# Two transformer layers on one core: the first MLP block made of units 0 and 1, units 6 and 7 alone at the end

## The chip, the cores and the metric

The kernel runs on one core of a Trainium2 chip. Its time is the device time of one execution in microseconds (us); the figure quoted is the median of three runs. One execution was profiled as well, and its trace gives each instruction's start and duration on TensorE (PE; its weight loads are listed apart as PEld), VectorE (DVE), ScalarE (ACT), GpSimd (POOL) and on the queue of SyncE (SP), which issues the DMAs.

## What is computed

The input is 32 sequences of 64 tokens with 512 features, a condition vector for each sequence, and positions. Two layers follow each other, all in float32.

Layer 0 normalises by the root of the mean square, scaled by a projection of the condition, and applies attention with 8 query heads of 64, one key and value head, and rotary angles from the given positions. It adds the result to x, normalises again with a second scale, and applies the gated MLP, whose middle has 2048 features:

```
x = x + attention(ada_rms(x, cond)) @ Wo.T
h = ada_rms(x, cond)
x = x + (silu(h @ Wg.T) * (h @ Wu.T)) @ Wd.T
```

Layer 1 is attention alone: a layer norm with scale and shift from the condition, 16 query heads of 32, keys and values of 4 heads through a latent of 128, a window mask that hides nothing within 64 tokens, a softmax, an output projection and the residual.

## The kernel before

**Units and blocks.** The 2048 tokens are eight units of 256 (four sequences each, `UT` = 256). Attention of both layers goes unit by unit: `attention0(u, room)` (line 689) is layer 0 up to the MLP's input, `attention1(u, room)` (line 858) is layer 1. The MLP of layer 0 goes by blocks of one or two units: `BLOCKS = ((0,), (1, 2), (3, 4), (5, 6), (7,))`.

**The MLP.** Each weight matrix is cut into eight sets of 2x2 quarters, and the 2x2 product is made with seven products in place of eight; this needs sums of weight quarters, sums of input quarters, and sums of the products. For each of 24 sets (gate, up and down, eight each) a block issues 7 x 2 matmul calls, and each float32 call stands in the trace as two instructions, so 28. Their moving operand has 256 columns if the block has two units and 128 if it has one; the weights are read whole either way. Products P1, P6, P5, P7 come first (`EARLIER`, `gate_up_first`), P2, P3, P4 later (`gate_up_last`); `partial`, `silu` and `gated` empty PSUM (L1063 to L1105), `down` adds to x.

**Weights.** Sets are read again for every block, through four slots (`MW` = 4). In the first block the quarters come from `in_wmlp`, and `sums_of_set` (L331 to L334) makes four sums of them: three on VectorE (on GpSimd for the first two sets) and one on GpSimd. The sums are written to HBM (`sums`, L342 and L344), 512 KB for each set as are the quarters read; later blocks read three quarters and four sums (`load_part`, L296 to L302).

**Sums of the input.** The last unit of a block makes T1, T3, T2 and T4 at the end of its `attention0` (L850 to L853) on VectorE. In a block of one unit they are of halves of its tokens, in a block of two they are of the two units. Product P1 needs only the first unit's h, P6 needs T2.

**The opening.** Units 0 and 1 are interleaved by hand before the planner starts. `FIRST` is a string: "a" takes the next piece of unit 0's `attention0`, "b" of unit 1's, "m" a piece of the modulations (projections of the condition), "i" issues two idle matmul calls on a constant, "r" a square root that brings the table of Sqrt into ScalarE, and "|" marks VectorE's latest instruction, behind which the sums of sets 2 to 4 must come. Within this loop TensorE keeps the order of issue; the other engines' order is settled by the scheduler of the tile framework, which goes by priority and by what is ready. Units 0 and 1 run in a "lean" form, with more, shorter pieces and statistics by quarters. A piece ends at each `yield cost, latency`.

**Angles.** Cosine and sine of units 0 and 1 are made first (`first_angles`); `angles(units, apart)` (L410) makes them for two units at a time in eight pieces of VectorE and ScalarE work (L424 and L428 to L449). `turning` walks over `TURNED`, units (2, 3), (4, 5), (6, 7), as a job of the planner. There is one buffer for positions.

**The planner.** After the opening, `Order.run` (L81) picks the next piece of the job that is furthest behind (`done / total`) and is ready. In round j the jobs are the block's MLP, `attention0` of the next block's units (`in_turn`), what is left of unit 1 (`ahead`) and of the angles, and from round 1 on `chain`, layer 1 of units 0 to 5 in turn; its total is 0.8 x 24 for each unit of the block before. A round ends when the MLP and the next block's `attention0` are done. Unit 6's layer 1 begins within the last round (four pieces), and the end is again a hand-written string, `LAST`, of units 6 and 7. Five buffers hold x, so x of units 5, 6 and 7 is loaded after layer 1 of units 0, 1 and 2.

Of the kernel before, what the change touches and what calls it, by code (L numbers as in the profile page):

```python
# [1 line left out]

# [1 line left out]

# [7 lines left out]
I32 = mybir.dt.int32  # L12
AF = mybir.ActivationFunctionType
ALU = mybir.AluOpType
# [30 lines left out]
TURN = (0.15911865234375, 3.628432750701904e-05, 6.4192136051133275e-09, 1.4247115856860781e-12)  # L45
ROUND = 12582912.0
WARM = 11
STAY = 13854 - 4 * 128 + 4 * 128 + 4 * 256 + 128 + 4 * 7 * 256 + 4 * 7 * 256
FIRST = "aaaaaaa bb a mm aa bb a bbb aa b mm a bb r aa a m b a bi m b i a | b".replace(" ", "")
EARLY = 4  # L50
TURNED = ((2, 3), (4, 5), (6, 7))
BLOCKS = ((0,), (1, 2), (3, 4), (5, 6), (7,))
GROUPS = ((0, 1, 2, 3), (4, 5, 6, 7))
H2 = 4
MODS = 4
# [76 lines left out]
def two_blocks(ctx: ExitStack, tc: tile.TileContext, a: dict, out: bass.AP):  # L132
# [87 lines left out]
    nc.gpsimd.memset(quarter, float(np.float32(np.pi / 2)))  # L220

    positions = []
    pos_slot = fixed([P, 2 * S])

    def load_positions(units):
        t = pos_slot.bitcast(I32)[:, : len(units) * S]
        nc.sync.dma_start(t, a["pos"][:, units[0] * S : (units[-1] + 1) * S])
        positions.append(t)

    first_loads = ExitStack()  # L230
    first_loads.enter_context(ordered(tc, mybir.EngineType.SP))
    load_positions((0, 1))
    small = fixed([P, C_ALL])
    nc.sync.dma_start(small, a["small"])
    condT = small[:, C_COND:C_VECS].rearrange("p (k b) -> p k b", b=B)
# [174 lines left out]
    def angles(units, apart):  # L410

        n = len(units) * S
        cols = slice(units[0] * S, units[0] * S + n)
        posi = positions.pop()
        big = work("many", [P, 10 * n], f"many_{units[0]}", 1)
        prods, rnds = (big[:, i * 5 * n : (i + 1) * 5 * n].rearrange("p (k c) -> p k c", c=n) for i in range(2))
        few = work("some", [P, 9 * n], f"some_{units[0]}", 1).rearrange("p (k c) -> p k c", c=n)
        posf, ang, lo, hi, acc, sign, f, size, sine = (few[:, k] for k in range(9))
        v, c = nc.vector, nc.scalar

        def group(*steps):
            with after(tc, mybir.EngineType.DVE, latest(tc, mybir.EngineType.DVE)):
                for op, *args in steps:
                    op(*args)  # L424
            return 0.0, apart

# [12 lines left out]
        yield group((v.tensor_tensor, prods, prods, rnds, ALU.subtract))  # L439
        yield group((v.tensor_reduce, acc, prods.rearrange("p k c -> p c k"), AX.X, ALU.add))  # L440
        yield group(
            (v.scalar_tensor_tensor, acc, lo, TURN[2], acc, ALU.mult, ALU.add),
            (v.scalar_tensor_tensor, acc, ang, TURN[3], acc, ALU.mult, ALU.add),
            (v.tensor_scalar, rnds[:, 0], acc, ROUND, ROUND, ALU.add, ALU.subtract),
            (v.tensor_tensor, f, acc, rnds[:, 0], ALU.subtract),
        )
        c.activation(size, f, AF.Abs)
        c.activation(angle[:, 0, cols], size, AF.Sin, scale=-TWO_PI, bias=quarter)
        c.activation(sine, f, AF.Sin, scale=TWO_PI)  # L449
        turned_units.update(units)  # L450
        yield group((v.tensor_tensor, angle[:, 1, cols], sine, sign, ALU.mult))

    def turning():
        for i, units in enumerate(TURNED):
            yield from angles(units, 4.0 if i else 2.0)
            if i + 1 < len(TURNED):
                load_positions(TURNED[i + 1])

    def first_angles(u):

# [132 lines left out]
    def rms(u, s, h, room, name):  # L593

        x = x_units[u]
        lean = "lean" in room
        sq = tile4(room, "h", f"sq_{name}") if lean else work("sq", [P, KC, UT], f"sq_{name}", 1)

        with after(tc, mybir.EngineType.Activation, roots[-1]) if name == "a2" else nullcontext():
            nc.scalar.activation(sq, x, AF.Square)  # L600
        if lean:
            parts = [sq[:, k] for k in range(KC)]
            c = KC // 2

# [83 lines left out]

    def attention0(u, room):
        kb, vb = kblk0[u % 2], vblk0[u % 2]  # L690
        lean = "lean" in room
        h = tile4(room, "h", f"h0_{u}")

        def query(i):

            q = abank(f"q0_{u}_{i}").rearrange("p (c t) -> p c t", c=2)
            for c in range(2):
                project(q[:, c], wqkv[i], slice(c * P, (c + 1) * P), h)
            two = [P, 2, UT]

            def turn(cos, sin):
# [14 lines left out]
        if lean:  # L716
# [8 lines left out]
            turn = query(0)  # L725
            yield 3.4, 0.0

        if lean:
# [1 line left out]
        else:  # L730
# [1 line left out]
        yield 1.0, 0.0  # L732

        qT = tile4(room, "qT", f"qT0_{u}")
        turn = turn or query(0)
        turn(cos, sin)
        yield 0.0 if lean else 3.4, 0.0

        kv = kv or keys_values()
        ku = work("u", [P, 512], f"ku_{u}")[:HD0, :UT]  # L740
        kw = work("v", [P, 512], f"kw_{u}")[:HD0, :UT]
        nc.vector.tensor_tensor(kw, kv[:HD0, :UT], sin[:HD0], ALU.mult)
        nc.vector.tensor_tensor(ku, kv[:HD0, :UT], cos[:HD0], ALU.mult)
        nc.vector.stream_shuffle(kw, kw, OTHER)

        vT = work("vT", [P, US, 2, S], f"vT_{u}", 1)
        twice = [HD0, US, 2, S]
        nc.vector.tensor_tensor(
            vT[HD0:],
            kv[HD0:, :UT].rearrange("p (b s) -> p b s", s=S).unsqueeze(2).to_broadcast(twice),  # L750
            r[HD0:].rearrange("p (b s) -> p b s", s=S).unsqueeze(2).to_broadcast(twice),
            ALU.mult,
        )

        ku, kw = (t.rearrange("p (b s) -> p b s", s=S) for t in (ku, kw))
        nc.vector.tensor_tensor(kb[:HD0], ku, kw, ALU.add)
        nc.scalar.copy(kb[HD0:], kb[:HD0])
        yield 0.0 if lean else 1.7, 0.0

        query(1)(cos, sin)  # L760
        yield 3.4, 0.0

        vt = abank(f"vt_{u}").rearrange("p (b d) -> p b d", d=P)
# [442 lines left out]
    homes["now"] = everywhere  # L1206
    for u in range(2):
        first_angles(u)
    positions.pop()
    for _ in modulation(0):  # L1210
        pass
    load_positions(TURNED[0])
    load_sets(2)
    load_mod(2)
    load_mod(3)

    first = work("p0", [P, 1024], "p0_0", 1)

    ahead = Job(attention0(1, {"ring": "1", "lean": True}), A0)
    streams = {  # L1220
        "a": attention0(0, {"ring": "0", "lean": True, "p": [first[:, :512], first[:, 512:]]}),
        "b": ahead.pieces,
        "m": other_mods(),
    }
    with ordered(tc, mybir.EngineType.PE):
        for name in FIRST:
# [7 lines left out]
                roots.append(latest(tc, mybir.EngineType.Activation))  # L1234
            else:
                next(streams[name], None)
    rest = [ahead, Job(turning(), 1.0)]
    for w, key in ((wq1, "wq1"), (wkd, "wkd"), (wkv1, "wkv1"), (wo1, "wo1")):
        nc.sync.dma_start(w, a[key])
    for u in range(2, XB):  # L1240
        load_x(u)
    combine(0)
    combine(1)
# [30 lines left out]
            if not n:  # L1274
                return

    def in_turn(units):
        for u in units:
            while u not in x_units or u not in turned_units:
                yield 0.0, 1.0  # L1280
            yield from attention0(u, {"ring": "0"})

    chain = Job(behind(), 0.8 * A1)
    for j, units in enumerate(BLOCKS):
        now = Job(mlp(j), M * len(units))
        jobs = [now, *rest]
        must = [now]
        if j == 0:
            must.append(ahead)
        if j + 1 < len(BLOCKS):  # L1290
            more = [u for u in BLOCKS[j + 1] if u > 1]
            must.append(Job(in_turn(more), A0 * len(more)))
            jobs.append(must[-1])
        if j == 1:
            jobs.append(chain)
# [108 lines left out]
```

## Time and profile before

| What | us |
|---|---|
| median of 3 runs (998.87 to 1000.03) | 999.79 |
| the profiled execution, its own time | 1000.52 |
| its span, first to last instruction | 998.7 |
| TensorE busy in the span (98%) | 975.1 |
| weight loads, beside the matmuls (85%) | 852.4 |
| VectorE busy (53%) | 530.1 |
| GpSimd busy (43%) | 428.2 |
| ScalarE busy (30%) | 302.0 |
| mean granted TensorE clock | 0.997 of full |
| moved by DMA, 132.23 MB | 132 GB/s over the span |

A busy share is a mean over stages that differ. The span falls into an opening (0 to 62.3 us, units 0 and 1), a first MLP block of one unit (to some 171 us, where the next block's first product appears; its last down product ends near 184), three blocks of two units (to 842.8), a last block of one unit (to 946.3) and a tail in which only layer 1 of units 6 and 7 is left. A matmul row in the timeline gives its start, how long the group took, line, operation, tiles, shape and count, and in brackets the idle time before it with what ended it. The matmuls of the MLP start 0.112 us apart with 128 columns and 0.216 us apart with 256.

### The profile page before, as it was taken

Reading aid. Unit: us, or ns where it says so; the run is one execution under the profiler, and the core shown is the slowest. Engines: PE = TensorE matmul, PEld = TensorE weight load, DVE = VectorE, ACT = ScalarE, POOL = GpSimd, SP = SyncE. Lnnn points to the kernel's source line nnn. Section 1 sums busy time; section 2 is a strip of 40 time slices with the busy share of each in tenths; the row PEclk is TensorE's granted clock in tenths of the full one; section 3 lists DMA queues with packets and bytes.
Section 4 is the critical chain, followed back from the end, with each engine's and each line's share of the span. In section 5 each row is a group of like instructions: output and inputs, shape, how many; then the busy total and the mean of one; then the engine's idle time right before and its main releaser. Section 6 shows DMA issues by size and latency. Waiting matters only on the chain.

```text
span 998.7 us, 17463 instructions
## 1 busy us (share of the span) xinstructions
PE 975.1 (98%) x6710; PEld 852.4 (85%) x6710; DVE 530.1 (53%) x1119; ACT 302.0 (30%) x560; POOL 428.2 (43%) x439
## 2 busy tenths in 40 slices
PE   8899988999999999999999999999999999999998
PEld 7788988888888888887888888888788889999986
DVE  5658787654373442655246372455334643654274
ACT  4453233223214210225214251222313330423132
POOL 3336257335433334435343352454325343844252
PEclk9999999999999999999999999999999999999999
DMA  7837376624222445223232234333323335745401
GB/s 269 310 117 239 130 248 196 208 92 134 69 69 80 137 139 173 90 80 110 78 108 88 73 132 138 115 106 106 96 86 105 132 109 168 246 149 190 138 1 43
DMA packets 82642, 132.23 MB, mean 132 GB/s; under 512 B 8832, under 2 KB 48512, under 8 KB 82176
## 3 DMA queue, kind: packets, MB, share of 16 engines
q1 hardware_dynamic: 82560, 131.12, 39.5%
q8 instruction: 53, 0.87, 0.4%
q14 instruction: 29, 0.24, 0.1%
HBM read 114.31 MB, written 16.78 MB: 131 GB/s over the span
## 4 chain that ended last, share of the span: by engine, by line
PE 87%; DMA 4%; DVE 3%; ACT 1%; POOL 1%; issue 1%; SPq 1%; POOLq 0%; DVEq 0%; ACTq 0%
PE gu L1048 38%; PE down L1048 17%; PE po L626 11%; PE q L626 10%; DMA stays<-in_wmlp 2%; PE pp L661 2%; PE sc L974 2%; PE lat L626 1%; PE kv L626 1%; ACT cT L815 1%; PE cx L805 1%; PE cx L1005 1%; PE sc L784 1%; DMA mod<-in_mod 1%; PE tab L494 1%
## 5 line engine op out<-in xcount | busy, mean ns | idle before, releaser
L1048 PE MATMUL gu<-h,stays 128*128 128x256 f32 (+1 forms) x1280 | 258.5, 340 | 5.9 <-issue 5.2
L1048 PEld LDWEIGHTS gu<-h,stays 128*128 128x128 f32 x1280 | 208.0, 191 | 30.4 <-issue 7.4
L1048 PE MATMUL down<-stays 128*128 128x256 f32 (+1 forms) x1120 | 208.4, 339 | 0.3 <-DVE stays L332 0.3
L1048 PE MATMUL gu<-hc,stays 128*128 128x256 f32 (+1 forms) x960 | 195.4, 338 | 2.8 <-DVE stays L332 2.8
L1048 PEld LDWEIGHTS down<-stays 128*128 128x128 f32 x1120 | 177.2, 190 | 22.4 <-issue 3.6
L1048 PEld LDWEIGHTS gu<-hc,stays 128*128 128x128 f32 x960 | 157.4, 191 | 18.4 <-DVE stays L332 3.0
L626 PE MATMUL q<-h,stays 128*128 128x256 f32 x480 | 110.7, 384 | 0.0
L626 PE MATMUL po<-cT,stays 128*128 128x256 f32 x480 | 107.9, 380 | 1.0 <-ACT cT L815 0.8
L1104 POOL TENSOR_TENSOR stays<-gate,stays 128x768 f32<-128x768 f32 (+1 forms) x40 | 53.8, 1346 | 114.7 <-DVE stays L1093 103.2
L626 PEld LDWEIGHTS po<-cT,stays 128*128 128x128 f32 x480 | 90.3, 190 | 14.4 <-ACT cT L815 2.4
L626 PEld LDWEIGHTS q<-h,stays 128*128 128x128 f32 x480 | 91.4, 192 | 12.6
L1063 ACT COPY e<-gu 128x256 f32<-128x256 f32 (+1 forms) x80 | 26.2, 328 | 172.5 <-PE gu L1048 169.7
L637 POOL TENSOR_TENSOR qT<-u_q,v_q 128x512 f32<-128x512 f32 x30 | 38.2, 1275 | 86.1 <-DVE v_q L636 82.9
L656 POOL TENSOR_TENSOR p<-p,sm 128x512 f32<-128x512 f32 x40 | 41.5, 1057 | 72.3 <-DVE sm L655 66.0
L682 DVE TENSOR_TENSOR x<-x,po 128x512 f32<-128x512 f32 x28 | 19.2, 686 | 90.7 <-PE po L626 90.7
L1064 DVE TENSOR_TENSOR u<-e,gu 128x256 f32<-128x256 f32 (+1 forms) x80 | 28.6, 358 | 53.2 <-ACT e L1063 53.0
L613 POOL TENSOR_TENSOR h<-x,stays 128x1024 f32<-128x1024 f32 x12 | 23.1, 1929 | 68.4 <-DVE x L682 38.4
L1105 POOL TENSOR_TENSOR stays<-stays 128x512 f32<-128x512 f32 (+1 forms) x40 | 45.0, 1126 | 2.9
L568 DVE RECIPROCAL stays<-stays 128x256 f32<-128x256 f32 (+1 forms) x23 | 35.4, 1540 | 19.7 <-ACT stays L567 19.5
L1065 DVE TENSOR_TENSOR w<-u,gu 128x256 f32<-128x256 f32 (+1 forms) x80 | 29.1, 364 | 30.8 <-PE gu L1048 29.6
L1151 POOL TENSOR_TENSOR x<-x,c 128x256 f32<-128x256 f32 x16 | 12.1, 758 | 74.3 <-DVE c L1138 74.3
L1093 DVE TENSOR_TENSOR gate<-gu,u 128x512 f32<-128x512 f32 (+1 forms) x40 | 23.3, 582 | 32.8 <-PE gu L1048 32.5
(230 smaller groups left out, 1266.2 us busy)
## 6 DMA issues: line engine op xcount, KB each, us to landing
stays<-sums SPq DMA_DIRECT2D x96, 384.0 KB, 3.0
stays<-in_wmlp SPq DMA_DIRECT2D x120, 256.0 KB, 2.9
stays<-in_wmlp SPq DMA_DIRECT2D x120, 128.0 KB, 2.5
stays<-sums SPq DMA_DIRECT2D x96, 128.0 KB, 2.3
sums<-stays SPq DMA_DIRECT2D x24, 384.0 KB, 3.8
mod<-in_mod SPq DMA_DIRECT2D x8, 512.0 KB, 6.3
x<-in_x SPq DMA_DIRECT2D x8, 512.0 KB, 6.2
a<-in_wmlp SPq DMA_DIRECT2D x24, 128.0 KB, 3.8
```

The source lines that it names most:

```text
L568: nc.vector.reciprocal(r, r)
L613: nc.gpsimd.tensor_tensor(by_seq(h), by_seq(x), per_seq(s, u), ALU.mult)
L626: nc.tensor.matmul(ps, w[:, k, cols], h[:, k, :], start=(k == 0), stop=(k == KC - 1))
L637: nc.gpsimd.tensor_tensor(dst, u, v, ALU.add)
L656: nc.gpsimd.tensor_tensor(p8, p8, sm.unsqueeze(2).to_broadcast(wide), ALU.mult)
L1048: nc.tensor.matmul(ps[REGION[p]][:, c], w[:, slot, cols], moving, start=opening and ps.opens(p, c, k), stop=p in LATER, skip_group_check=True,
L1063: nc.scalar.copy(e, ps[0])
L1064: nc.vector.tensor_tensor(u2, e, ps[1], ALU.add)
L1065: nc.vector.tensor_tensor(w2, u2, ps[2], ALU.add)
L1093: nc.vector.tensor_tensor(c12_21, ps.late_pair()[:, :, 0], u2.to_broadcast([P, 2, ht]), ALU.add)
L1104: e.tensor_tensor(act[:, 2:5], gate[:, 1:4], act[:, 2:5], ALU.mult)
L1105: e.tensor_tensor(act[:, 0:4:2], act[:, 2:4], act[:, 1:3], ALU.subtract)
```

## The change

The first block takes units 0 and 1, and the units alone are 6 and 7, both at the end. Unit 1's `attention0` ends within the opening. In its place the planner's round 0 has the rest of unit 2 and then unit 3, which `AHEAD` lists by round; rounds 1 and 2 prepare (4, 5) and (6, 7), and the last two rounds prepare nothing. The opening string has two new letters: "t" takes the eight pieces of the angles of units 2 and 3, and "c" takes six pieces of unit 2's `attention0`, to the first half of its second pair of queries. The string's two "i" are gone, and "|" stands ahead of unit 1's output.

Unit 2 runs in a "split" form: keys and values come before the first queries, and each pair of queries can be broken after its first half. It has its own two rows for its statistics (`own`). The order of instructions in other units is the same. The positions have two buffers, the second load stands among the first loads, and x of unit 2 is loaded right behind the modulation weights. In `angles`, Abs and the two Sin must come behind ScalarE's latest instruction; unit 2's second square no longer has to come behind the last root.

```diff
-FIRST = "aaaaaaa bb a mm aa bb a bbb aa b mm a bb r aa a m b a bi m b i a | b".replace(" ", "")
+FIRST = "aaaa ttt aaa bb a tttt mm aa t bb a bbb c aa b mm a bb r aa b c bb m a b c | b a b c b a b c m b c".replace(" ", "")
-BLOCKS = ((0,), (1, 2), (3, 4), (5, 6), (7,))
+BLOCKS = ((0, 1), (2, 3), (4, 5), (6,), (7,))
+AHEAD = ((3,), (4, 5), (6, 7), (), ())
...
-    pos_slot = fixed([P, 2 * S])
+    pos_slots = [fixed([P, 2 * S]) for i in range(2)]
...
     load_positions((0, 1))
+    load_positions(TURNED[0])
...
-        c.activation(size, f, AF.Abs)
-        c.activation(angle[:, 0, cols], size, AF.Sin, scale=-TWO_PI, bias=quarter)
-        c.activation(sine, f, AF.Sin, scale=TWO_PI)
+        with after(tc, mybir.EngineType.Activation, latest(tc, mybir.EngineType.Activation)):
+            c.activation(size, f, AF.Abs)
+            c.activation(angle[:, 0, cols], size, AF.Sin, scale=-TWO_PI, bias=quarter)
+            c.activation(sine, f, AF.Sin, scale=TWO_PI)
...
         for i, units in enumerate(TURNED):
-            yield from angles(units, 4.0 if i else 2.0)
-            if i + 1 < len(TURNED):
-                load_positions(TURNED[i + 1])
+            if i:
+                load_positions(units)
+                yield 0.0, 4.0
+            yield from angles(units, 4.0)
...
-        with after(tc, mybir.EngineType.Activation, roots[-1]) if name == "a2" else nullcontext():
-            nc.scalar.activation(sq, x, AF.Square)
+        nc.scalar.activation(sq, x, AF.Square)
...
                 project(q[:, c], wqkv[i], slice(c * P, (c + 1) * P), h)
+                if split and not c:
+                    yield 1.7, 0.0
...
+        if split:
+            vT = keys(keys_values())
+            yield 1.7, 0.0
+        turn = turn or (yield from query(0))
         turn(cos, sin)
         yield 0.0 if lean else 3.4, 0.0
...
+        if not split:
+            vT = keys(kv or keys_values())
+            yield 0.0 if lean else 1.7, 0.0
+
+        (yield from query(1))(cos, sin)
...
-    load_positions(TURNED[0])
     load_sets(2)
     load_mod(2)
     load_mod(3)
+    load_x(2)
...
+    own = [fixed([P, UT]) for i in range(2)]
...
+    turns = turning()
+    third = attention0(2, {"ring": "0", "split": True, "r": own})
...
-        "b": ahead.pieces,
+        "b": attention0(1, {"ring": "1", "lean": True}),
+        "c": third,
         "m": other_mods(),
+        "t": turns,
...
-    rest = [ahead, Job(turning(), 1.0)]
+    rest = [Job(turns, 1.0)]
...
-    for u in range(2, XB):
+    for u in range(3, XB):
         load_x(u)
...
-        if j == 0:
-            must.append(ahead)
-        if j + 1 < len(BLOCKS):
-            more = [u for u in BLOCKS[j + 1] if u > 1]
-            must.append(Job(in_turn(more), A0 * len(more)))
+        if AHEAD[j]:
+            more = in_turn(AHEAD[j])
+            if j == 0:
+                more = chain_of(third, more)
+            must.append(Job(more, A0 * len(AHEAD[j]) + 12.0 * (j == 0)))
             jobs.append(must[-1])
```

More of the change, by code (lines that the diff above doesn't have):

```diff
@@ L1 @@
 from contextlib import ExitStack, contextmanager, nullcontext
+from itertools import chain as chain_of
 import numpy as np
@@ L47 @@
 WARM = 11
[L48 to L49 removed]
+STAY = 13854 + 128 + 2 * 256 - 4 * 128 + 4 * 128 + 4 * 256 + 128 + 4 * 7 * 256 + 4 * 7 * 256
+FIRST = "aaaa ttt aaa bb a tttt mm aa t bb a bbb c aa b mm a bb r aa b c bb m a b c | b a b c b a b c m b c".replace(" ", "")
 EARLY = 4
 TURNED = ((2, 3), (4, 5), (6, 7))
[L52 removed]
+BLOCKS = ((0, 1), (2, 3), (4, 5), (6,), (7,))
+AHEAD = ((3,), (4, 5), (6, 7), (), ())
 GROUPS = ((0, 1, 2, 3), (4, 5, 6, 7))
@@ L222, in two_blocks @@
     positions = []
-    pos_slot = fixed([P, 2 * S])
+    pos_slots = [fixed([P, 2 * S]) for i in range(2)]
     def load_positions(units):
-        t = pos_slot.bitcast(I32)[:, : len(units) * S]
+        t = pos_slots[units[0] // 2 % 2].bitcast(I32)[:, : len(units) * S]
         nc.sync.dma_start(t, a["pos"][:, units[0] * S : (units[-1] + 1) * S])
@@ L413, in angles @@
         cols = slice(units[0] * S, units[0] * S + n)
-        posi = positions.pop()
+        posi = positions.pop(0)
         big = work("many", [P, 10 * n], f"many_{units[0]}", 1)
@@ L690, in attention0 @@
         kb, vb = kblk0[u % 2], vblk0[u % 2]
-        lean = "lean" in room
+        lean, split = "lean" in room, "split" in room
         h = tile4(room, "h", f"h0_{u}")
@@ L724, in attention0 @@
             yield 1.7, 0.0
-            turn = query(0)
+            turn = yield from query(0)
             yield 3.4, 0.0
@@ L734, in attention0, with keys @@
         qT = tile4(room, "qT", f"qT0_{u}")
-        turn = turn or query(0)
+        def keys(kv):
+            ku = work("u", [P, 512], f"ku_{u}")[:HD0, :UT]
+            kw = work("v", [P, 512], f"kw_{u}")[:HD0, :UT]
+            nc.vector.tensor_tensor(kw, kv[:HD0, :UT], sin[:HD0], ALU.mult)
+            nc.vector.tensor_tensor(ku, kv[:HD0, :UT], cos[:HD0], ALU.mult)
+            nc.vector.stream_shuffle(kw, kw, OTHER)
+            vT = work("vT", [P, US, 2, S], f"vT_{u}", 1)
+            twice = [HD0, US, 2, S]
+            nc.vector.tensor_tensor(
+                vT[HD0:],
+                kv[HD0:, :UT].rearrange("p (b s) -> p b s", s=S).unsqueeze(2).to_broadcast(twice),
+                r[HD0:].rearrange("p (b s) -> p b s", s=S).unsqueeze(2).to_broadcast(twice),
+                ALU.mult,
+            )
+            ku, kw = (t.rearrange("p (b s) -> p b s", s=S) for t in (ku, kw))
+            nc.vector.tensor_tensor(kb[:HD0], ku, kw, ALU.add)
+            nc.scalar.copy(kb[HD0:], kb[:HD0])
+            return vT
+        if split:
+            vT = keys(keys_values())
+            yield 1.7, 0.0
+        turn = turn or (yield from query(0))
         turn(cos, sin)
         yield 0.0 if lean else 3.4, 0.0
[L739 to L760, printed above, removed]
+        if not split:
+            vT = keys(kv or keys_values())
+            yield 0.0 if lean else 1.7, 0.0
+        (yield from query(1))(cos, sin)
         yield 3.4, 0.0
@@ L1208, in two_blocks @@
         first_angles(u)
-    positions.pop()
+    positions.pop(0)
     for _ in modulation(0):
         pass
-    load_positions(TURNED[0])
     load_sets(2)
@@ L1215, in two_blocks, with in_turn @@
     load_mod(3)
+    load_x(2)
     first = work("p0", [P, 1024], "p0_0", 1)
-    ahead = Job(attention0(1, {"ring": "1", "lean": True}), A0)
+    own = [fixed([P, UT]) for i in range(2)]
+    def in_turn(units):
+        for u in units:
+            while u not in x_units or u not in turned_units:
+                yield 0.0, 1.0
+            yield from attention0(u, {"ring": "0"})
+    turns = turning()
+    third = attention0(2, {"ring": "0", "split": True, "r": own})
     streams = {
         "a": attention0(0, {"ring": "0", "lean": True, "p": [first[:, :512], first[:, 512:]]}),
-        "b": ahead.pieces,
+        "b": attention0(1, {"ring": "1", "lean": True}),
+        "c": third,
         "m": other_mods(),
+        "t": turns,
     }
@@ L1236, in two_blocks @@
                 next(streams[name], None)
-    rest = [ahead, Job(turning(), 1.0)]
+    for pieces in (streams[name] for name in "abm"):
+        assert next(pieces, None) is None
+    rest = [Job(turns, 1.0)]
     for w, key in ((wq1, "wq1"), (wkd, "wkd"), (wkv1, "wkv1"), (wo1, "wo1")):
         nc.sync.dma_start(w, a[key])
-    for u in range(2, XB):
+    for u in range(3, XB):
         load_x(u)
@@ L1275, in some @@
                 return
[L1277 to L1281, printed above, removed]
     chain = Job(behind(), 0.8 * A1)
```

## The prediction

> **What bounds the kernel now.** I read the page first, then busy time by stage, then TensorE's instructions in order of time, then the chain that ended last.
>
> ```profile
> span 998.7 us, 17463 instructions
> ...
> PE 975.1 (98%) x6710; PEld 852.4 (85%) x6710; DVE 530.1 (53%) x1119; ACT 302.0 (30%) x560; POOL 428.2 (43%) x439
> ```
>
> TensorE bounds the whole, so a change can win only where PE is idle or slow. I cut the span at the first MLP matmul (62.3), where block (1,2)'s first matmul appears (171.3), and where the later blocks start; the last cut is the tail.
>
> ```profile
> core 0: us, PE busy (x) PEld busy (x) DVE busy (x) ACT busy (x) POOL busy (x), PEclk, DMA share, GB/s
> 0.00:62.30 62.30, 54.43 (x607) 44.50 (x607) 35.34 (x91) 29.77 (x69) 26.42 (x42) 0.97 0.69 244
> 62.30:171.30 109.00, 100.82 (x846) 95.16 (x847) 88.79 (x210) 38.26 (x88) 54.59 (x65) 0.98 0.60 198
> 171.30:392.00 220.70, 220.32 (x1295) 190.70 (x1295) 107.68 (x209) 56.47 (x95) 86.01 (x81) 1.00 0.38 124
> ```
>
> PE idles 7.9 us in the opening, 8.2 us in the first block and 0.4 us in the next; there DVE falls from 81% to 49%. The PE rows of the first block with a wait:
>
> ```profile
> 95.63 1.13 PE L1048 MATMUL gu<-h,stays 128*128 128x128 f32 x8 [1.71 <-issue]
> ...
> 130.51 1.16 PE L1048 MATMUL gu<-hc,stays 128*128 128x128 f32 x8 [2.76 <-DVE stays L332]
> ...
> 163.86 2.04 PE L1048 MATMUL gu<-h,stays 128*128 128x128 f32 x8 [2.64 <-issue]
> ```
>
> The bracket is the wait ahead of the row. With four smaller ones (0.25, 0.33, 0.49 and 0.28; the 0.70 at the block's start I count to the opening) the block loses 8.46 us. The chain says where the first two of the long ones come from:
>
> ```profile
> 90.05 4.56 DMA stays<-in_wmlp
> ...
> 124.71 4.40 DMA a<-in_wmlp
> ...
> 129.51 0.95 DVE stays L332
> ```
>
> A weight set lands, DVE makes its sums (L331 to L333), the matmul follows. For a single unit, a set is 28 matmuls of 128 columns, 3.1 us (PE rows 72 in 8.04 us, 0.112 each). In that time DVE owes it three sums (12.9, 11.0 and 13.9 us over 22 sets: 1.7 us) and its share of the emptying of PSUM: of L1064, L1065 and L1084, 0.29 each, one 0.42 and half a 0.28 (1.4 us). That is 3.1 us of DVE for 3.1 us of PE, with unit 2's attention and the angles on top; and 1 MB of DMA (512 KB in, 512 KB of sums out), 330 GB/s, where 198 were moved. The last wait also costs clock: the eight matmuls at 163.86 take 2.04 us instead of 1.05, and the granted clock over 163 to 167 us is 0.61, 1.6 us at no progress. Lost: 8.46 + 1.6 = **10.1 us**.
>
> **The change, part by part.** (1) *First block a pair.* A set is now 28 matmuls of 256 columns at 0.216 us (16 in 3.45), 6.05 us, while the three sums stay 1.7 us and the emptying becomes some 2.1 us (three of 0.42, one of 512 columns at 0.69, half of 0.42): 3.8 us of DVE in 6.05, and 1 MB in 6.05 us, 173 GB/s. Both stand below what 842.8 to 946.3 carries without a wait for weights (188 GB/s, shown at D). I keep 0.6 us of the 10.1: **-9.5**. Bounds: at worst the waits halve only, as the load does (-5); at best all go (-10.1). The number of single and paired blocks is unchanged (two and three), so PE's matmul work is the same.
>
> (2) *More work ahead of that MLP.* Moved before it: unit 1's output (32 x 0.216 = 6.9), its statistics and row (0.65 + 1.0), and of unit 2 the mean (0.43), tables (0.9), keys (1.73) and three quarters of the queries (24 x 0.216 = 5.2). 16.8 us move, none is added; the MLP starts near 79. Its two "i" (eight idle matmuls of 0.112) go: **-0.9**.
>
> (3) *Angles of units 2 and 3 in the opening.* The rows of one pass sum to 6.2 us of DVE (18.6 over three), ACT to some 3.6, with one more table load of 1.28 for Sin and one back to Exp. DVE idles 2.73 us before 20.2, 0.83 before 28.4, 1.85 before 30.6 and 3.17 before 38.1. The first three operations fit; the last four groups, 4.2 us, stand ahead of unit 0's softmax in 2.7 us of idle: 1.5 us late. Unit 1's queries and tables (31.0 to 37.8 on PE) hide it to the transposes at 37.83, which wait for POOL's product that ended at 36.97: **+0.5**. From below 0; without the cover 1.5 + 1.28 = +2.8.
>
> On the table: the trace has it at 28.01 for 1.28 us, and other loads are followed by their activation 0.01 to 0.02 us later. [...]
>
> (4) *The end of the opening.* Now the MLP's second product needs unit 1's sums: last projection, x (0.69), square (1.06), statistics (0.65), root (0.32), reciprocal (0.55), row (1.0), product (1.22), three subtractions of 512 columns (0.69 each): 7.6 us, and some eight hand-overs of about 0.15. Beside it PE has unit 2's half queries (3 x 1.73), unit 0's row (1.0), its own 1.65, a transpose (0.1) and the first product (4 x 0.216 = 0.9): 8.8 us against 8.8. I take 1.1 us of wait, and 0.9 where a context waits for its copy. Gone are the waits of 0.35 and 0.70 in unit 0's end: **+1.0**. Bounds: -1.0; or DVE first turns a query (2.1) and makes three sets' sums (3 x 1.7, since "|" lets them start earlier): 7.2 us of wait, the 0.9, and a halved clock of 1.6 as at 163, less the 1.05: +8.7.
>
> On the clock: over 31 to 36 us it is 0.69, after a longest idle of 1.28. [...]
>
> (5) *Units 6 and 7 alone, one after the other.* The block of unit 6 carries two second-layer attentions (units 4 and 5) in some 115 us instead of 210 to 240. The single block now (842.8 to 946.3) shows what one costs: waits for POOL of 0.32 and 0.67. One attention more beside a single block: **+1.0**, bounds 0 to 3. That chain is long in latency, but the next MLP does not wait for it. Loads of x for units 5 to 7 hang on the attentions of units 0 to 2, which run with the same shares as units 1 and 2 do now (loads at 504 and 617, a wait of 0.74): nothing.
>
> (6) *Second position buffer, unit 2's own rows, loads moved on SP* (x of unit 2, positions): x already starts at 28.8 and is used after 40; the weights behind it are wanted at 79. Nothing; at worst the 6.2 us of one x landing, hidden by the later start. No change of the sum.
>
> **Sum.** -9.5 - 0.9 + 0.5 + 1.0 + 1.0 = -7.9. The profiled execution took 1000.52 (span 998.7): 992.6. The median of the runs is 0.73 lower, so **991.9**.
>
> **Rivals.** *A, the forecast* (0.57): 988.5 to 995.5.
>
> *B, the opening's end is exposed* (0.15): part (4) at its upper bound, 991.9 + 7.7 = 999.6, from 996 to 1003. For it: DVE is in every link and the order of its queue is not fixed here; against: in unit 0's end the same links leave PE waiting 1.05.
>
> *C, the opening gains* (0.12): unit 2's work also fills the older waits (28.05, 30.04, 45.24 and 47.77: 0.41 + 1.28 + 0.78 + 0.67 = 3.1) and the halved clock at 31 goes (1.6), and part (4) costs nothing: 991.9 - 4.7 - 1.0 = 986.2. Against: most unit 2 pieces come after 45 us.
>
> *E, the change doesn't do what it says* (0.08): the first block's waits hang on the order of loads and sums and not on the rate, 5 us stay: 991.9 + 4.5 = 996.4.
>
> *D, slower* (0.08): unit 7's block is starved of weights. It loses filler: of 28 us (103.5 less 24 x 3.14) I expect 10 to remain, unit 6's early pieces (costs of 3.5) and what is left of units 4 and 5 (costs of 45, of which the planner places 38.4 before). So 24 sets of 0.92 MB, 22.0 MB, are wanted in 75 + 10 = 85 us. Four sets are in the slots; 18.3 MB must land in about 82 us, 223 GB/s. The stage now averages 188; were that a ceiling, the block would take 15 us more: 1007. It undoes the gain below 203 GB/s. Against it:
>
> ```profile
> 842.80:946.30 103.50, 102.52 (x888) 98.12 (x887) 49.44 (x124) 29.19 (x64) 52.19 (x62) 1.00 0.58 188
> 860.00:870.00 10.00, 9.04 (x75) 8.39 (x74) 7.22 (x11) 6.08 (x10) 7.99 (x9) 1.00 0.84 271
> ```
>
> At 188 GB/s the queues are 58% busy, at 271 84%, and PE waited for no weights.
>
> **Numbers.** A measurement tells 0.2%, 2.0 us, from no change: faster is below 997.8, slower above 1001.8. Faster: A 0.57, C 0.12, E 0.06, B 0.04, together 0.79. Same: B 0.08, E 0.02, D 0.01: 0.11. Slower: B 0.03, D 0.07: 0.10. Range 986.5 to 1000.5: left out are half of C (0.06), B's top (0.05) and D (0.08).
>
> **What would show it.** Right: the MLP starts near 79; the first block (about 145 + 12 + 20 us) shows PE idle under 1.5 us, no L331 to L333 in front of PE, full clock. (3) is wrong if unit 0's transposes come later than 38.5; (4) if PE waits over 2 us for DVE's h or hc at the first MLP; (5) if the last two blocks idle over 3 us. The forecast fails if the clock halves at the MLP's start or the weights of unit 7 appear in the chain.

## The result, and the profile after

| What | before | after |
|---|---|---|
| median of the runs compared, us | 999.91 (6 runs, 998.87 to 1002.44) | 1006.92 (6 runs, 1004.7 to 1009.15) |
| ratio after to before, 95% interval | | 1.0067 [1.0047, 1.0086] |
| the profiled execution, us (its span) | 1000.52 (998.7) | 1006.68 (1004.9) |

The change makes the kernel slower, by 7.0 us; the forecast was 8 us faster, and the time lies above the whole range. The page after:

```profile
span 1004.9 us, 17433 instructions
...
PE 977.5 (97%) x6702; PEld 851.0 (85%) x6702; DVE 537.9 (54%) x1119; ACT 303.9 (30%) x562; POOL 426.9 (42%) x439
```

The work is the same, less eight idle matmuls. Of the 6.2 us that the span grew by, 2.4 stand in PE's busy time and 3.8 in its idle time. By stage (us; busy time and count of PE, PEld, DVE, ACT, POOL; granted clock, DMA share, GB/s), cut at the first MLP matmul of each block, and the first block at 256, where its weight sums end:

```profile
0.00:79.90 79.90, 69.12 (x712) 57.84 (x713) 53.98 (x126) 37.68 (x87) 30.59 (x46) 0.98 0.60 208
79.90:256.00 176.10, 168.65 (x915) 142.55 (x914) 119.40 (x222) 48.17 (x89) 81.92 (x78) 0.99 0.36 118
...
271.20:509.20 238.00, 237.08 (x1414) 202.05 (x1413) 117.51 (x224) 74.84 (x117) 99.90 (x91) 1.00 0.33 102
```

In the first block PE still idles 7.5 us, with DVE busy 68% of the time (82% before, over 62.3 to 182.3) and 118 GB/s moved (203 before). Both loads fell as forecast, and the waits stayed.

Idle time alone leaves out slow clock, and that matmuls right behind a wait took longer (four of 256 columns 1.13 us at 189.17, 1.03 at 187.15). So I took every matmul's distance to the next one's start, less the distance at which the same form streams undisturbed (0.216 us for 256 columns, 0.112 for 128; the fastest seen for the others), and summed this **loss** by stage. All losses below are counted so.

| Loss, us | before | after | difference |
|---|---|---|---|
| opening | 15.6 | 17.4 | +1.8 |
| first block | 14.1 | 13.9 | -0.2 |
| the four blocks behind | 3.5, 7.8, 2.4, 2.0 (15.7) | 7.4, 8.2, 1.8, 2.3 (19.7) | +4.0 |
| tail | 6.8 | 8.0 | +1.2 |
| idle matmuls dropped | | | -0.9 |

The sum is +5.9, the spans differ by 6.2. Four of PE's ten waits in the first block, the three longest among them (the bracket is the wait ahead of the row):

```profile
184.46 1.13 PE L1062 MATMUL gu<-h,stays 128*128 128x256 f32 x4 [0.59 <-DVE x L1167]
...
189.17 1.13 PE L1062 MATMUL gu<-h,stays 128*128 128x256 f32 x4 [0.99 <-DVE u L1078]
191.31 1.10 PE L1062 MATMUL gu<-h,stays 128*128 128x256 f32 x4 [1.01 <-DVE gate L1098]
...
252.61 5.60 PE L1062 MATMUL down<-stays 128*128 128x256 f32 x17 [2.02 <-DVE stays L335]
```

PE's waits there are all put down to DVE, and of their 7.5 us only 2.0 to a sum of weights (L335); the rest is the emptying of PSUM (L1078, L1098, L1107, L1116) and the addition to x (L1167). What DVE itself waited for, in the first block of the kernel before (62 to 184 us) and after (80 to 257; total, times, longest):

```profile
DVE stays L331 <- DMA stays<-in_wmlp: 8.7, 6, 2.2
DVE stays L333 <- DMA a<-in_wmlp: 3.8, 4, 2.0
```

```profile
DVE stays L334 <- DMA stays<-in_wmlp: 23.8, 17, 3.9
```

DVE stands for 23.8 us at the first sum of a set whose quarters have not landed. Its instructions there, in order:

```profile
186.52 0.43 DVE L334 TENSOR_TENSOR stays<-a,stays 128x256 f32<-128x256 f32 x1 [1.45 <-DMA stays<-in_wmlp]
186.98 0.43 DVE L335 TENSOR_TENSOR stays<-stays 128x256 f32<-128x256 f32 x1
187.32 1.27 DVE L658 TENSOR_REDUCE sm<-p 128x8 f32<-128x512 f32 x2
188.51 0.32 DVE L659 RECIPROCAL sm<-sm 128x8 f32<-128x8 f32 x2
188.75 0.37 DVE L1078 TENSOR_TENSOR u<-e,gu 128x256 f32<-128x256 f32 x1
...
246.88 0.43 DVE L334 TENSOR_TENSOR stays<-a,stays 128x256 f32<-128x256 f32 x1 [3.92 <-DMA stays<-in_wmlp]
...
247.82 0.69 DVE L1107 TENSOR_TENSOR stays<-gu,u 128x512 f32<-128x512 f32 x1
...
250.98 1.48 DVE L335 TENSOR_TENSOR stays<-stays 128x256 f32<-128x256 f32 x1
```

The rows show DVE keeping the order of its queue: at 246.88 it has stood for 3.92 us, and L1107, whose products PE had finished at 243.3, comes only behind the sum. L335 of the same set follows at 250.98, and PE waits 2.02 us for it. At 186.52 less was held up: ScalarE's exponentials, which the softmax's sum (L658) reads, ended at 186.08 and 186.60, and its copy for the emptying (L1078) at 186.86. So only 0.4 of the 1.45 us held ready work, and L334 and L335 themselves held it up to 187.3; PE then waited 0.99 for L1078 and 1.01 for L1098. Nobody needed that sum yet: counted by 28 MLP matmuls a set, its set begins on PE at 201.15. I call this distance, from the start of a set's first sum to the set's first matmul, its lead; its median over sets 2 to 23 is 12.0 us here and 4.9 in the kernel before.

The chain of waits tells why the quarters are late (start, length, what):

```profile
176.57 3.86 DMA stays<-in_wmlp
180.46 0.44 DVE stays L334
180.92 0.44 DVE stays L335
181.48 0.80 POOL stays L337
182.70 3.79 DMA stays<-in_wmlp
186.52 0.44 DVE stays L334
```

Two rows of SP's queue between them:

```profile
182.29 0.32 SPq L345 DMA_DIRECT2D sums<-stays  x1
182.70 0.41 SPq L303 DMA_DIRECT2D stays<-in_wmlp  x1
```

This turn reads as a ring: a load lands, the sums are made, their write is issued (L345), and behind it on the same queue the next load (L303), which takes 3.8 us. One turn takes 6.06 us, as long as a set on PE (6.05).

**Theory:** the first block loses its time to the order on DVE's queue. A sum is put ahead of work that is due, and waits there for a landing. **Rivals:** DVE is too busy; the DMA can't carry it; the moved pieces in the opening cost it.

### The profile page after: what moved, and what is told of

It is laid out like the page before. It is cut to its first block, busy times and chain, and to the rows that moved or that the text cites. A ratio compares the mean times of both kernels' runs of the same rounds, so it can differ in the third digit from the quotient of the medians.

```text
span 1004.9 us, 17433 instructions
## 1 busy us (share of the span) xinstructions
PE 977.5 (97%) x6702; PEld 851.0 (85%) x6702; DVE 537.9 (54%) x1119; ACT 303.9 (30%) x562; POOL 426.9 (42%) x439
## 4 chain that ended last, share of the span: by engine, by line
PE 85%; DVE 6%; DMA 4%; ACT 2%; POOL 1%; issue 1%; SPq 0%; POOLq 0%; DVEq 0%; ACTq 0%
PE gu L1062 35%; PE down L1062 17%; PE q L630 11%; PE po L630 10%; DMA stays<-in_wmlp 2%; PE pp L665 2%; PE sc L988 2%; PE lat L630 1%; PE kv L630 1%; PE cx L819 1%; PE cx L1019 1%; DMA stays<-in_wqkv 1%; ACT cT L829 1%; DVE stays L334 1%; PE tab L499 1%
## 5 line engine op out<-in xcount | busy, mean ns | idle before, releaser
L630 PEld LDWEIGHTS q<-h,stays 128*128 128x128 f32 x480 | 91.2, 192 | 12.5
L641 POOL TENSOR_TENSOR qT<-u_q,v_q 128x512 f32<-128x512 f32 x30 | 38.2, 1275 | 78.0 <-DVE v_q L640 70.6
L686 DVE TENSOR_TENSOR x<-x,po 128x512 f32<-128x512 f32 x28 | 19.2, 686 | 81.7 <-PE po L630 81.6
L1078 DVE TENSOR_TENSOR u<-e,gu 128x256 f32<-128x256 f32 (+1 forms) x80 | 28.8, 360 | 62.9 <-ACT e L1077 62.8
L1167 DVE TENSOR_TENSOR x<-x,down 128x256 f32<-128x256 f32 x48 | 18.0, 416 | 43.7 <-PE down L1062 43.7
L1169 POOL TENSOR_TENSOR x<-x,u_d 128x256 f32<-128x256 f32 x32 | 22.4, 725 | 40.2 <-DVE x L1167 40.1
```

The lines of the kernel that those rows point to most:

```text
L630: nc.tensor.matmul(ps, w[:, k, cols], h[:, k, :], start=(k == 0), stop=(k == KC - 1))
L641: nc.gpsimd.tensor_tensor(dst, u, v, ALU.add)
L1078: nc.vector.tensor_tensor(u2, e, ps[1], ALU.add)
L1169: nc.gpsimd.tensor_tensor(to, to, more, ALU.add)
```

## The experiments

Where nothing else is said, a diff is against the kernel after. "Waits for landings" are those of DVE at the first sum in the first block (80 to 257 us).

**The sums one set later.** The three places that call for sums ask for one set less ahead.

```diff
-        combine(place[what] + 2)
+        combine(place[what] + 1)
...
-                    combine(place[what] + 3)
+                    combine(place[what] + 2)
```

> Theory 1 (an in-order queue): in the first block VectorE stands at the sums of a set whose quarters have not landed yet, and the emptying of PSUM behind it makes TensorE wait; the planner issues the sums two sets ahead, just behind the product that frees the slot. Theory 2 (work): VectorE and ScalarE have too much to do in bursts there, attention and angles beside the sums. Here the sums are issued one set later, all work unchanged. Theory 1: VectorE's waits for landing quarters fall from 23.8 us to under 6, the first block loses 5 to 7 us in place of 13.9, time 998 to 1001. Theory 2: nothing is taken away, 1005 to 1008.

1004.76 us, 1.0058 [1.0036, 1.0079]. Waits for landings 21.5, first block 10.4. The call comes later, but the scheduler, free to order DVE, put the sums back to the same places: the median lead is 12.0 us, as without the edit. The edit failed to do what it was for; it tells only that the place of the call isn't the place in the queue.

**Sums of data that are already there**, and **no sums at all**. The first keeps every instruction and DMA and reads a resident weight in the place of the quarters; the second loads the slots of the sums by DMA.

```diff
-            e.tensor_tensor(f[:, 0], a21, l[:, 1], ALU.add)
...
+            w0, w1, w2, w3 = (wo0[:, k, :256] for k in range(4))
+            e.tensor_tensor(f[:, 0], w0, w1, ALU.add)
```

> The first block's sums are made from weights that lie in SBUF from the opening on (output weights of layer 0) in place of the set's own quarters, so the products of the MLP are not the reference's; the same instructions in the same places and the same DMAs, but no wait for a landing. Theory 1: 998 to 1001, as with the later issue. Theory 2: 1005 to 1008, since VectorE does the same work.

> The first block's sums are left out (0.42 us or more each, three on VectorE and one on GpSimd for each of 24 sets), and the four quarters that they would fill are loaded by DMA instead, as later blocks load them. Theory 1: 997 to 1000, little better than the two kernels that only take the wait away. Theory 2: about a third of VectorE's work in the block is gone, 1002 to 1005. If the first block were bounded by DMA: 1007 or more, since 128 KB a set more are moved.

Resident: 999.06, 0.9996 [0.998, 1.0012]. Its first block, over the same window as above:

```profile
79.90:256.00 176.10, 174.21 (x960) 149.82 (x959) 128.11 (x233) 48.72 (x91) 84.03 (x79) 1.00 0.33 115
```

DVE is busier (128 us for 119, as the block got further), the DMA moves as much (115 GB/s), and PE idles 1.9 us in place of 7.5. The block loses 4.9 for 13.9: 9.0 us, near the 9.5 of the forecast. The kernel's time shows less of it, as its opening loses 20.6 with a loss of 5.18 behind POOL at 30.0. Without sums: 993.14, 0.9937 [0.9915, 0.9959], first block 2.0, so 2.9 us are what the sums cost by being there (I had expected 997 or more). A busy DVE and a full DMA are refuted for this block; the wait for landings is left.

**The new blocks alone.** The blocks of after with the opening of before (and the rest of unit 1 behind it); units 2 and 3 and the angles wholly in the planner.

```diff
-FIRST = "aaaa ttt aaa bb a tttt mm aa t bb a bbb c aa b mm a bb r aa b c bb m a b c | b a b c b a b c m b c".replace(" ", "")
+FIRST = "aaaaaaa bb a mm aa bb a bbb aa b mm a bb r aa a m b a bi m b i a b bbbbb |".replace(" ", "")
-AHEAD = ((3,), (4, 5), (6, 7), (), ())
+AHEAD = ((2, 3), (4, 5), (6, 7), (), ())
```

> The new blocks alone: the opening has only units 0 and 1 (with the two pairs of idle matmuls), then unit 1's last pieces without cover; unit 2 and the angles of units 2 and 3 are left to the planner. Theory 1: the first block still loses 13 us or more, the end of the opening some 4 to 7 more than with unit 2's pieces beside it: 1009 to 1014. Theory 2, or if the angles and unit 2's pieces in the opening are what costs: 1000 to 1006.

1006.43, 1.0077 [1.0053, 1.0101]: the same as after. I expected it slower. The opening loses 18.1, the first block 15.2, each some 1 us more than after. That reads as if the moved pieces were worth nothing; two kernels further down show otherwise.

**The writes of the sums on another queue**: on GpSimd's, and on ScalarE's, so that no load stands behind a write.

```diff
-                nc.sync.dma_start(to[:, 0:3], sets["f"][n][:, 0:3])
+                nc.scalar.dma_start(to[:, 0:3], sets["f"][n][:, 0:3])
```

> Why do the quarters land late? Theory 1a: SyncE's queue is in order too, and the writes of a set's sums to HBM (which wait for VectorE and GpSimd) stand ahead of the loads of other sets, so that landing, sums, write and next load form a ring of about 6 us a set, as long as the 6.05 us of TensorE. Theory 1b: the loads wait for TensorE to free the slot, and VectorE's queue has the sums too early for what is loaded so late. Here the writes are issued by GpSimd. 1a: the first block loses 5 to 8 us in place of 13.9, time 998 to 1002, if issuing costs GpSimd no more than 1 us a write. 1b: 1004 to 1008.

> The same writes issued by ScalarE. 1a: SyncE's loads are free, but ScalarE's queue now stands before writes that wait for the sums, with the copies that empty PSUM behind them: between 998 and 1005. 1b: 1004 to 1008.

On ScalarE: 1003.06, 1.003 [1.0018, 1.0043], first block 9.7.

```profile
DVE stays L334 <- DMA stays<-in_wmlp: 17.2, 16, 2.2
```

On GpSimd: waits for landings 14.6, first block 12.5, opening 23.0; 1009.83, 1.0094 [1.0066, 1.0122]. The waits fall by a quarter to two fifths: the shared queue of SP is a part of the ring, not its whole. On GpSimd the time lies above both expectations: PE still waits 2.5 for DVE's L1098, it waits 1.97 at 161.2 for a statistic that GpSimd makes (L561), and the opening loses 5.6 more than after.

**The sums late, and held there.** The calls of the first experiment, and each sum must come behind DVE's latest instruction at its call.

```diff
-            with after(tc, mybir.EngineType.DVE, marks[0]) if 2 <= n < 5 else nullcontext():
+            with after(tc, mybir.EngineType.DVE, latest(tc, mybir.EngineType.DVE)) if n >= 2 else nullcontext():
```

> The sums one set later, and besides each set's sums must stand behind VectorE's instructions that were issued before them, so that the scheduler can't move them forward. Theory 1 in either form: VectorE's waits for landings fall under 8 us of 23.8, the first block loses 5 to 8 us: 998 to 1001. If a later place makes TensorE wait for the sums themselves, the wait comes back as matmuls behind L335: 1003 to 1008.

995.85, 0.9961 [0.9947, 0.9976]. DVE's waits for landings in the first block (80 to 247 us), and its window up to where the sums end:

```profile
DVE stays L334 <- DMA stays<-in_wmlp: 2.1, 1, 2.1
```

```profile
79.80:245.80 166.00, 164.73 (x913) 141.93 (x912) 116.97 (x226) 48.38 (x89) 80.99 (x79) 1.00 0.40 130
```

The waits go, the median lead falls to 5.4 us, the stretch with the same sums takes 166.0 us in place of 176.1, and the block loses 3.8: 10.3 less than before the change. The other stages stay as in after (17.3; 7.5, 7.5, 1.8, 2.3; 8.0). No instruction was taken away and the loads of quarters take no less (a median of 3.0 us for 256 KB in both): the order alone was worth 11 us (10.6 by the ratios to the kernel before, which ran beside each). This version beats both kernels.

**All sums on GpSimd.**

```diff
-            e = nc.gpsimd if n < 2 else nc.vector
+            e = nc.gpsimd
```

> All sums of the first block on GpSimd (0.64 us each instead of 0.42). Theory 1: VectorE no longer stands in front of a landing, GpSimd does, and behind it stand the products that only the later down projection needs: 995 to 1001. Theory 2, or if GpSimd becomes the bound (82 us busy of 177, some 42 more): 1003 to 1010.

1005.11, 1.005 [1.0032, 1.0069], first block 10.1. The same wait has moved to the other queue (GpSimd's waits, 80 to 257 us):

```profile
POOL stays L334 <- DMA stays<-in_wmlp: 21.8, 9, 4.3
```

PE no longer waits for the emptying on DVE. It waits 3.2 us for the statistic of L561, behind GpSimd's queue, and the granted clock behind it is 0.57 over 155 to 159 us. The theory had 995 to 1001; the time fell where the rival had it, because GpSimd's queue too holds work that PE waits for.

**The same order in the kernel before**, that is, with one unit in the first block (later calls and held sums, against the kernel before).

> The kernel before with its own blocks and opening, and only the sums' new place (one set later, fixed behind what VectorE was given before). If the queue's order is the whole cause, its first block too falls from 14.1 us of loss to 5 or less: 990 to 993. If the rate argument of the prediction holds beside it (3.1 us of VectorE for 3.1 us of TensorE with a unit alone), the first block keeps 9 us or more: 994 to 1000.

1004.81, 1.0045 [1.0029, 1.0061]: slower, and above both expectations. The landing waits fall to 1.3, yet the first block loses 19.2 for 14.1. PE's waits there (60 to 188 us):

```profile
PE pp L661 <- POOL p L656: 3.1, 2, 2.6
PE gu L1048 <- issue: 3.0, 1, 3.0
PE gu L1048 <- ACT some L449: 1.7, 1, 1.7
```

Here DVE is busy 105.1 of 126.4 us (83%). The median lead is only 1.6 us; PE waits behind the softmax's product (L656), for 3.0 us that the profile puts to no engine, and behind ScalarE's work on the angles (L449), and the granted clock is 0.75 over 129 to 133 us and 0.69 over 167 to 171. So this order gains nothing in a block of one unit. That agrees with what the forecast said of the rate, but does not prove it: no other order was tried there.

**The new blocks alone, with the sums held** (the fourth experiment's edit and the order), and **unit 2's pieces taken out of the opening again**, with the angles left there (against the kernel with the sums held):

```diff
-FIRST = "aaaa ttt aaa bb a tttt mm aa t bb a bbb c aa b mm a bb r aa b c bb m a b c | b a b c b a b c m b c".replace(" ", "")
+FIRST = "aaaa ttt aaa bb a tttt mm aa t bb a bbb aa b mm a bb r aa b bb m a b | b a b b a b m b".replace(" ", "")
...
-    third = attention0(2, {"ring": "0", "split": True, "r": own})
+    third = attention0(2, {"ring": "0"})
...
-            must.append(Job(more, A0 * len(AHEAD[j]) + 12.0 * (j == 0)))
+            must.append(Job(more, A0 * (len(AHEAD[j]) + (j == 0))))
```

> The new blocks with the old opening (unit 1's last pieces uncovered, unit 2 and the angles left to the planner), and the sums' new place. Against the changed kernel with the sums' new place (995.9): the end of the opening waits 4 to 5 us more and the first block has the angles: 998 to 1003. If the new pieces in the opening cost more than they cover: 992 to 995.

> x7_lead1_order with unit 2's pieces taken out of the opening again (the whole of its attention is left to the planner, in its usual form); the angles of units 2 and 3 stay in the opening. Theory 'the angles in the first block are what costs 17.8 us' (they are 18.6 us of VectorE work, the last unit's statistics wait behind them): the first block still loses about 4 us, the opening up to 4 us more than 17.3 because unit 1's end is uncovered, 996 to 1000. Theory 'unit 2's attention costs it' (its work in the opening covers the end of unit 1, and in the block its own waits come on top): opening and block together lose 15 us more, 1008 to 1014. In between, 1000 to 1008, both carry a part.

1013.62, 1.0126 [1.0106, 1.0147], and 1008.28, 1.0083 [1.0069, 1.0097]. The first is over 10 us above what I expected. With the sums in place the pieces in the opening are worth 17.8 us (1013.62 less 995.85): some 12.4 by unit 2's attention, 5.3 by the angles. These runs did not stand side by side; by their ratios to the kernel before, which did run beside each, it is 16.5, 12.2 and 4.3. Unit 2's pieces cover the end of unit 1: without them PE loses 1.94 there behind ScalarE's copy and 1.19 behind a square, and the first block loses 12.9 for 3.8. DVE in it, without unit 2's pieces ahead:

```profile
186.64 1.27 DVE L658 TENSOR_REDUCE sm<-p 128x8 f32<-128x512 f32 x2
187.83 0.32 DVE L659 RECIPROCAL sm<-sm 128x8 f32<-128x8 f32 x2
188.06 0.38 DVE L334 TENSOR_TENSOR stays<-a,stays 128x256 f32<-128x256 f32 x1
188.36 1.26 DVE L336 TENSOR_TENSOR stays<-stays,a 128x256 f32<-128x256 f32 x1
```

The sum comes at once, but late, behind a softmax; PE waits 1.37 for L334. So the fourth experiment's "worth nothing" was the queue's order hiding one effect with another: holding the sums costs 7.2 us where DVE has much else to do (1006.43 to 1013.62) and gains 11.1 where it hasn't (1006.92 to 995.85); by the ratios 4.9 and 10.6.

**The angles later in the opening**, **the lone block second**, **the second layer spread wider** (three separate edits, each against the kernel with the sums held; the second also lets round 0 go on with unit 2):

```diff
-FIRST = "aaaa ttt aaa bb a tttt mm aa t bb a bbb c aa b mm a bb r aa b c bb m a b c | b a b c b a b c m b c".replace(" ", "")
+FIRST = "aaaa ttt aaa bb a mm aa bb a bbb tttt t c aa b mm a bb r aa b c bb m a b c | b a b c b a b c m b c".replace(" ", "")
...
-BLOCKS = ((0, 1), (2, 3), (4, 5), (6,), (7,))
-AHEAD = ((3,), (4, 5), (6, 7), (), ())
+BLOCKS = ((0, 1), (2,), (3, 4), (5, 6), (7,))
+AHEAD = ((), (3, 4), (5, 6), (7,), ())
...
-        chain.total = 0.8 * A1 * (len(BLOCKS[j - 1]) if j else 1)
+        chain.total = 1.1 * A1 * (len(BLOCKS[j - 1]) if j else 1)
```

> The changed kernel with the sums' new place, and the last five pieces of the angles in the opening behind unit 1's second queries instead of ahead of unit 0's softmax. The prediction's step on the angles says 0.5 us; the profile after shows TensorE waiting 1.8 us for unit 0's softmax, and half a clock window behind it. If that wait is the angles': 992 to 994.5. If it is GpSimd's sums of the first two sets: 995.5 to 997.

> The changed kernel with the sums' new place and the blocks (0, 1), (2), (3, 4), (5, 6), (7): the unit alone comes second instead of last but one. The blocks behind the first lost 15.7 us before and 19.7 after the change. If the place of the units alone at the end is the cause, 2 to 4 us come back, 992 to 994. If the loss goes with the amount of attention beside a block, it is 995 to 997, or more if a unit alone has too little time for two first-layer attentions: up to 1002.

> x7_lead1_order with the planner's total for the second layer's attentions at 1.1 in place of 0.8, so that they are spread wider. Theory 'blocks with two first-layer and two second-layer attentions lose 7.5 us each because the latter are packed too closely': the two blocks lose 5 to 6 each, 992 to 994, unless work is left for the tail, which would then be longer by as much. Rival 'the waits come from GpSimd's share and not from the spacing': the losses stay at 7 to 8, 995 to 997, or the tail grows and the time goes to 998 to 1002.

Angles later: 997.51, 0.9967 [0.9954, 0.9981]. The loss of 1.97 ahead of unit 0's transposes at 36 us goes, and the opening still loses 20.1 for 17.3, with a new loss of 1.69 at 58: the angles cause that wait, and it is not to be had for nothing. The total, above both expectations, shows no gain. Lone block second: 994.73, 0.994 [0.9918, 0.9961]; the blocks behind the first lose 17.8 for 19.1. Spread wider: 994.54, 0.9941 [0.9927, 0.9955]; the two pairs lose 6.5 and 8.7, together 15.2 for 15.0. The spacing is not what they lose by. The intervals of the last two overlap with that of the kernel with the sums held; neither is shown to be better.

## Why the prediction was wrong

**The step that failed is part (1)**, the first block as a pair: -9.5 forecast, -0.2 measured. Its reckoning of rates held: DVE and DMA had the room it gave them, and even the size holds, for with the sums held in place the same block gives -10.3. What fails is the step from "Both stand below what 842.8 to 946.3 carries" to "I keep 0.6 us of the 10.1": it took spare time on DVE and DMA for the absence of waits. I read the waits of before (2.76 for L332, behind a weight load) as a rate exceeded, without asking what stood behind the sum on DVE. The bound was wrong for the same reason: "at worst the waits halve" is a bound on a load, and an order has no such bound. The lines shown then had it: a load in the chain, then a sum, then PE. The waits of DVE by releaser, 8.7 us at L331 for landings, would have shown that DVE, busy 81% of the time, also stood idle with work behind it.

Rival E named this mechanism, "the order of loads and sums and not on the rate", with a chance of 0.08 and 5 us of waits left, 996.4. Size and chance were both too small: the waits of DVE went from 8.7 to 23.8. PE's set got twice as long, and the sums then stood a median of 12.0 us ahead of their set in place of 4.9, where their quarters had not landed. Called one set later, they still stood at 12.0; why the scheduler puts them there isn't shown. That the order is the cause is (995.85).

The profiled time is 14.1 us off (1006.68 for 992.6). By the table of losses part (1) makes 9.3 of it, part (5) 3.0, the tail 1.2, and (3) and (4) together 0.3.

**(2)** Idle matmuls -0.9, and the MLP at 79.9 for "near 79": right.

**(3) and (4)** The opening, forecast +0.5 and +1.0, measured +1.8 together. That the sum is so near is luck, for the parts differ and cancel: the end of unit 1 is covered (no loss over 0.27 at one matmul from 62.3 to 79.9), so B is refuted, while unit 0's transposes wait 1.80 for POOL's product, ahead of which no loss over 0.25 stood before; they start at 38.2, within the 38.5 that I allowed. A granted clock of 0.57 follows over 38 to 42 us, where before it was 0.69 over 31 to 36. C is refuted as well: the losses at 28 (1.8 for 1.48) and 46 (1.39 for 1.02) grew.

On the table of Sin: in the kernel after it loads at 36.36 for 1.28 us, and the activation starts at 37.65, 0.01 us behind it.

**(5)** Forecast +1.0, measured +4.0, outside its bounds of 0 to 3. The last two blocks lose little (1.8 and 2.3; the single block before lost 2.0), as forecast. What was not reckoned is that two pairs (7.4 and 8.2) now carry four attentions each, where before one did (7.8) and the others three (3.5 and 2.4). With the block orders of before and of after, a pair with four loses 6.5 to 8.7 in the kernels here and one with three 2.4 to 3.6; spreading them in time did not lower the sum. The number of attentions is not all of it either: with the lone block second, the pairs with three lose about 5 each. What in them PE loses beyond a statistic of POOL (0.94 and 1.46 us after, 0.90 before) stays open.

**(6)** Buffers and loads, nothing: no wait shows them. **D** is refuted: unit 7's block loses 2.3 us and the weights do not appear ahead of PE. **The tail** lost 1.2 more with the same work (6.8 to 8.1 in the kernels here). It wasn't forecast and isn't explained.

## What to carry to other kernels

When an engine is idle while its consumer waits for it, look at what the head of its queue waits for: here DVE, busy 68% of the time, stood 23.8 us at sums whose quarters had not landed, and work that was due stood behind some of them. A change that gives such an engine more room is only worth its reckoned rate if the order is fixed too; ask what a scheduler will move into the room. And judge parts of a change with that order held fixed, for here a shifted queue hid some 17 us of what a part was worth.

## What the runs showed of the hardware

Behind some of PE's waits the granted clock was low, behind others it was not. In the kernel after, around the wait of 2.02 at 252.6 (PE's busy time comes first, the clock stands third from the end):

```profile
250.00:254.00 4.00, 1.99 (x8) 1.41 (x7) 4.00 (x4) 0.00 (x0) 3.84 (x4) 0.93 0.17 68
253.00:257.00 4.00, 4.00 (x13) 3.20 (x12) 2.23 (x3) 0.00 (x0) 2.77 (x4) 0.57 0.79 276
```

With the angles later, around the loss of 1.69 at 58 us:

```profile
57.00:61.00 4.00, 2.47 (x15) 1.92 (x14) 2.56 (x6) 2.18 (x4) 2.55 (x3) 1.00 0.00 0
60.00:66.00 6.00, 5.38 (x69) 3.95 (x70) 2.57 (x3) 4.69 (x11) 1.87 (x2) 1.00 0.00 0
```

Another low stretch of the kernel after (0.57 over 38 to 42 us) stands behind a wait of 1.80, and with all sums on GpSimd one (0.57 over 155 to 159 us) behind a wait of 3.2. With the writes on GpSimd the clock was 1.00 over 161 to 165 us, behind a wait of 1.97. So in these runs the length of a wait alone does not tell the ones from the others, and what does isn't shown. A clock of 0.57 over 253 to 257 us is some 1.7 us at no progress (an estimate, 0.43 x 4), nearly as much as the wait ahead of it.
